# Weights of routed images one turn later, one branch for two rare cases, norms of tiles on GpSimd, constants of the scans from ScalarE's queue

## The chip, the cores and the metric

The kernel runs on one core of a Trainium2 chip. A core has five engines that run their own instruction streams side by side: TensorE (PE, matmuls; PEld are its weight loads), VectorE (DVE), ScalarE (ACT), GpSimd (POOL) and SyncE (SP, which here only issues DMAs). DMAs are issued from SP's, ACT's or POOL's queue. Each engine executes its own stream in order, so an instruction that waits for a semaphore holds up all that stand behind it on that engine. The metric is device time in microseconds from the first to the last instruction; lower is better.

## The reference

Two layers over an image batch `x` of shape (4, 256, 32, 32), all in float32. Each layer adds a token mixer to `x`, then a mixture of experts. The first layer's mixer is attention that keeps, in each row, only the `dyn_k` largest of 1024 scores; its mixture has 8 experts of 256 by 256, two for each token. The second layer's mixer is a selective scan in four directions; its experts are 256 by 1024. What matters here:

```python
attn = jnp.where(ranks < dyn_k, attn, -jnp.inf)
attn = jax.nn.softmax(attn, axis=-1)
...
rw, re = jax.lax.top_k(probs, TOP_K)
rw = rw / jnp.maximum(rw.sum(-1, keepdims=True), 1e-12)
...
h = jax.nn.gelu(tokens @ w1[e] + b1[e], approximate=False)
y = h @ w2[e] + b2[e]
out = out + combine[:, e:e + 1] * y
...
t = t + _L0_ffn_ref(_ln_t(t), ...)
```

`tokens` are layer-normalised rows; the two weights of a token come from the two largest router logits.

## The kernel before

**Order of stages.** (1) Attention of four images, with the first mixture's routing beside it; (2) a seam with two branches that are hardly ever taken; (3) the first mixture in 36 tiles of 256 tokens of one expert; (4) the scans; (5) the second mixture; (6) the output.

**Attention.** A half is 128 query rows of one group of four heads; there are 64. The loop `for i in range(len(order) + 8)` calls `turn(i)`; in a turn four halves stand at different steps (half i gets its scores, half i-3 its window and its masks), and one quarter of the weights of a pair of halves is exponentiated and multiplied with the values. The whole loop stands under `tc.manual_schedule()` (L1162): every engine gets its instructions in the order in which the code emits them. Work that is not of a half (projections, convolution, the routing) is cut into steps by generators. `plan(first, needed, steps, places)` enters them with a first place and a due turn, and `beside(i, place)`, called at five places of a turn, emits the next step of the one that is begun or due first. A step that yields True has put matmuls into the single PSUM bank of `bank(name)`; the next step reads them.

**Masks.** `Half.mask` (L810) makes four masks of 128x1024 on POOL (L814) in a turn. The matmuls of `Pair.weights` (L874) add them to the scores of both halves of a pair. After the masks POOL has `verify`, then whatever `behind_masks(i)` (L941) emits.

**Routing beside attention.** For images 0 to 2, `Routing0` starts its turns at `turn0 = 16 b + 24`. `feed` and `count` are planned steps. In turn 1 and 2 `spread` and `root` compute variance and reciprocal root on POOL (L290 to L311). `share` (L321, ACT, called in `before_masks` of turn 3) exponentiates the difference of two logits times that root. `shares` (L324, DVE) and `locate` (L331 to L337, POOL), in `behind_masks` of turn 3, make weights and slots; `fix` (L340, DVE, turn 4) rounds the slots; `send` (L212) writes one tile of 128 tokens a turn in turns 5 to 12 with two indirect DMAs from POOL, each of which waits for the one before.

**The last image** goes through `halved(b, h, ...)` for two halves of 512 tokens, and then `table` (L418 to L459, DVE), which lays out tiles: which expert and which block. The same function `halved` is used again in the first rare case. It reads: choose two experts (L361 to L380), count them by matmuls (`counted`), positions (L388 to L396), reciprocal root by three Newton steps (L397 to L403), Exp on ACT (L404), weights (L405 to L410); then eight sends for each half from POOL.

**The seam.** `bad` (L1387 to L1391) tests whether any row's threshold was ambiguous; `tc.If(again > 0)` (L1394) repeats attention by bits. Then constants are loaded (L1417 on ACT's queue; L1612 to L1617 five of the scans on SP's), b1 and b2 of the experts on SP's queue (L1812, L1814), and `tc.If(more_tiles > 0)` (L1901) runs tiles beyond 36. An If is a block that every engine passes; outside the manual part a scheduler orders the work between such blocks, in program order where things are ready.

**Tiles of the first mixture** (`Tile0`, from L1823): `load` (SP: rows xs, w1, w2), `normed` (L1846), `turned` (four transposes, L1853, one copy L1855), `small` (L1860 to L1871), `hidden` (eight matmuls L1878, Gelu L1880), `result` (eight matmuls L1886, L1889), `store` (L1893, L1895, and a DMA from POOL, L1897). Norms have two buffers (`pb`, bufs=2):

```python
nc.scalar.activation(self.xn[:, a], self.xs[:, a, :C], AF.Identity,
                     bias=self.xs[:, a, C + 3 : C + 4], scale=self.xs[:, a, C + 4 : C + 5])
```

Beside the tiles, six steps after each: from tile 14 on the 16 gathers of image 0's results (`fetched`, L1763, indirect DMAs from POOL), their transposes (`completed`), and the preparation of the scans (`Prep.steps`); from tile 22 on the gathers of image 1. In the scans and the rest nothing is changed.

Of the kernel before, what the change touches and what calls it, by code (L numbers as in the profile page):

```python
# [11 lines left out]
F32 = mybir.dt.float32  # L12
F16 = mybir.dt.float16
BF16 = mybir.dt.bfloat16
I32 = mybir.dt.int32
# [47 lines left out]
def metaformer(ctx: ExitStack, tc: tile.TileContext, t: dict, out: bass.AP):  # L63
# [123 lines left out]
    extra = cons.tile([1, 1], I32, tag="extra", name="extra")  # L187
    edges = cons.tile([P, PHASES, E], F32, tag="edges", name="edges")
# [153 lines left out]
    def halved(b, h, space, bank, wide_bank):  # L342
# [7 lines left out]
        ve, nm, rr, r0, red, m1, m2 = (room([M]) for _ in range(7))  # L350
# [17 lines left out]
        def best(value, hot):  # L368
# [7 lines left out]
        nc.vector.tensor_scalar(xr[b][:, four, C], red, -1.0, float(E), ALU.mult, ALU.add)  # L376
# [8 lines left out]
        yield True  # L385
        half = NHALF * b + h
        base = bases[:, half - 1] if half else region
        nc.vector.scalar_tensor_tensor(place_, sums[:, : M * E].rearrange("p (n e) -> p n e", e=E), float(C),  # L388
                                       base.unsqueeze(1).to_broadcast(wide), ALU.mult, ALU.add)
        nc.vector.scalar_tensor_tensor(bases[:, half], sums[:, NT * E : (NT + 1) * E], float(C), base,  # L390
                                       ALU.mult, ALU.add)
        yield False
        for k, hot in enumerate((hot1, hot2)):
            nc.vector.tensor_tensor(eq, hot, place_, ALU.mult)
            nc.vector.tensor_reduce(red, eq, AX.X, ALU.add)
            nc.vector.tensor_copy(here[:, k], red)  # L396
# [8 lines left out]
        nc.vector.scalar_tensor_tensor(xr[b][:, four, C + 3], nm, C ** 0.5, ve, ALU.mult, ALU.mult)  # L405
        nc.vector.tensor_copy(xr[b][:, four, C + 4], ve)
        nc.vector.tensor_scalar(red, m2, 1.0, None, ALU.add)
        nc.vector.reciprocal(m1, red)
        nc.vector.tensor_tensor(xr[b][:, four, C + 2], m2, m1, ALU.mult)
        nc.vector.tensor_tensor(xr[b][:, four, C + 1], m1, xr[b][:, four, C + 2], ALU.subtract)  # L410
        yield None

    def table(space, bank):
# [18 lines left out]
        nc.vector.tensor_scalar(extra, ends[0:1, V - 1 :], USUAL + 0.5, None, ALU.is_gt)  # L432

# [33 lines left out]
    with ExitStack() as st:  # L467
# [473 lines left out]
        def behind_masks(i):  # L941
            for turn0, routing in routings.items():
                at = i - turn0
                if at == 1:
                    routing.spread((0, 1))
                if at == 2:
                    routing.spread((2, 3))
                    routing.root()
                if at == 3:
                    routing.shares()  # L950
                    routing.locate()
                if at == 4:
                    routing.fix()
                if 5 <= at < 13:
                    send(routing.b, (at - 5,), None)

        def before_masks(i):
            for turn0, routing in routings.items():
                if i - turn0 == 3:
                    routing.share()  # L960

# [422 lines left out]
    bad = cons.tile([1, 1], I32, tag="bad", name="bad")  # L1384
    with tc.tile_pool(name="g_ps", bufs=1, space=PSUM) as pool_p, tc.tile_pool(name="g_sb", bufs=1) as pool_s:
        sure = pool_s.tile([P, 1], F32, tag="sure", name="sure")
        nc.vector.tensor_reduce(sure, fine, AX.XY, ALU.add)  # L1387
        nc.vector.tensor_scalar(sure, sure, 2.0 * (2 * B * NT) * 4 - 0.5, None, ALU.is_ge)
        tot = pool_p.tile([P, 1], F32, tag="tot", name="tot")
        nc.tensor.matmul(tot, mean_w, sure, start=True, stop=True)  # L1390
        nc.vector.tensor_scalar(bad, tot[0:1], (P - 0.5) / C, None, ALU.is_lt)  # L1391
    again = nc.values_load(bad[0:1, 0:1], min_val=0, max_val=1,
                           skip_runtime_bounds_check_because="a comparison gives 0 or 1")
    with tc.If(again > 0):  # L1394
        with ExitStack() as st:
            attention_by_bits(st)
        with tc.tile_pool(name="g_w", bufs=1) as pool_s, tc.tile_pool(name="g_ps", bufs=4, space=PSUM) as pool_p:
            nc.sync.dma_start(slots_x0.rearrange("(a p) c -> p a c", p=P),
                              blank(pool_s)[:, :W0].unsqueeze(1).to_broadcast([P, (E * BLOCKS + 1) * T // P, W0]))
            space = pool_s.tile([P, L], F32, tag="space", name="space")  # L1400
            for b in range(B):
                for h in range(NHALF):
                    wide_bank = pool_p.tile([P, L], F32, tag="w", name="wide_bank", bufs=2)
                    for _ in halved(b, h, space, lambda name: pool_p.tile([P, HALF], F32, tag="m", name=name),
                                    lambda: wide_bank):
                        pass
                    send(b, range(4 * h, 4 * h + 4), "scatter0_again")
            for _ in table(space, lambda name: pool_p.tile([P, HALF], F32, tag="m", name=name)):
                pass
# [202 lines left out]
    wd = load_rows(sw, "wd", C, nc.sync)  # L1612
    wbc = load_rows(sw, "wbc", 2 * NS, nc.sync)
    bd = load(sw, "bd", [P, CT], eng=nc.sync)
    dsk = load(sw, "dskip", [P, CT], eng=nc.sync)

    am = load(sw, "a_log", [P, CT, NS], eng=nc.sync)  # L1617
# [192 lines left out]
    with ExitStack() as st:  # L1810
        wp = st.enter_context(tc.tile_pool(name="m0_w", bufs=1))
        b1 = load(wp, "b1_0", [P, E, CT], eng=nc.sync)  # L1812
        b2 = wp.tile([P, E, C], F32, tag="b2_0", name="b2_0")
        nc.sync.dma_start(b2, t["b2_0"].rearrange("e d -> (e d)").partition_broadcast(P).rearrange(  # L1814
            "p (e d) -> p e d", e=E))
        pw = st.enter_context(tc.tile_pool(name="m0_e", bufs=4))
        pb = st.enter_context(tc.tile_pool(name="m0_b", bufs=2))
        ps_n = st.enter_context(tc.tile_pool(name="m0_ps_n", bufs=3, space=PSUM))
        ps1 = st.enter_context(tc.tile_pool(name="m0_ps1", bufs=1, space=PSUM))
        ps_h = st.enter_context(tc.tile_pool(name="m0_ps_h", bufs=2, space=PSUM))  # L1820
        blocks_x = slots_x0.rearrange("(k a p) c -> k p a c", a=T // P, p=P)

        class Tile0:  # L1823

            def __init__(self, i):
                self.i = i

            def register(self, k, most, engines):
                return nc.values_load(every_which[0:1, k, self.i : self.i + 1], engines=engines, min_val=0,
                                      max_val=most,  # L1830
                                      skip_runtime_bounds_check_because="the minimum with that of a count")

            def load(self):
                block = self.register(1, E * BLOCKS, [mybir.EngineType.SP])
                self.xs = pb.tile([P, T // P, W0], F32, tag="xs", name="xs", bufs=6)
                nc.sync.dma_start(self.xs, blocks_x[bass.ds(block, 1)].rearrange("o p a c -> p (o a) c"))
                e = self.register(0, E - 1, [mybir.EngineType.SP])
                self.w1 = pw.tile([P, CT, C], F32, tag="w1", name="w1")
                nc.sync.dma_start(self.w1, t["w1_0"][bass.ds(e, 1)].rearrange("o (c p) f -> p (o c) f", p=P))
                self.w2 = pw.tile([P, CT, C], F32, tag="w2", name="w2")  # L1840
                nc.sync.dma_start(self.w2, t["w2_0"][bass.ds(e, 1)].rearrange("o (c p) f -> p (o c) f", p=P))

            def normed(self):
                self.xn = pb.tile([P, T // P, C], F32, tag="xn", name="xn")
                for a in range(T // P):
                    nc.scalar.activation(self.xn[:, a], self.xs[:, a, :C], AF.Identity,  # L1846
                                         bias=self.xs[:, a, C + 3 : C + 4], scale=self.xs[:, a, C + 4 : C + 5])

            def turned(self):
                tp = ps1.tile([P, CT, T], F32, tag="tp", name="tp")  # L1850
                for a in range(T // P):
                    for c in range(CT):
                        nc.tensor.transpose(tp[:, c, ts(a, P)], self.xn[:, a, ts(c, P)], ident)  # L1853
                self.xe = pb.tile([P, CT, T], F32, tag="xe", name="xe")
                nc.vector.tensor_copy(self.xe, tp)  # L1855

            def small(self):
# [15 lines left out]
            def hidden(self):  # L1873
                hp = ps_h.tile([P, CT, T], F32, tag="hp", name="hp")
                self.hid = pb.tile([P, CT, T], F32, tag="hid", name="hid")
                for f in range(CT):
                    for c in range(CT):
                        nc.tensor.matmul(hp[:, f], self.w1[:, c, ts(f, P)], self.xe[:, c],  # L1878
                                         start=(c == 0), stop=(c == CT - 1))
# [479 lines left out]
```

## Time and profile before

| What | Value |
|---|---|
| Median of three runs (range) | 4113.35 us (4110.25 to 4118.84) |
| The profiled execution | 4111.36 us |
| Its span, granted TensorE clock | 4109.6 us, 0.876 |

The stages in the profiled execution, busy microseconds of each engine and the granted clock:

| Stretch, us from the start | Stage | PE | DVE | ACT | POOL | clock |
|---|---|---|---|---|---|---|
| 0 to 265 | start, pipeline of attention fills | 173.7 | 147.6 | 174.6 | 47.0 | 0.73 |
| 265 to 1960 | attention | 1367.0 | 1465.2 | 1479.5 | 967.6 | 0.78 |
| 1960 to 2031 | end of attention, seam | 33.2 | 32.6 | 14.0 | 18.6 | 0.70 |
| 2031 to 2253 | tiles of the first mixture | 186.8 | 145.1 | 134.8 | 72.1 | 0.95 |
| 2253 to 3521 | scans | 1228.1 | 1145.6 | 872.6 | 672.1 | 0.99 |
| 3521 to 4110 | second mixture, output | 546.3 | 104.6 | 166.3 | 94.3 | 0.96 |

Rows of the profile read thus: start in us from the span's start (in a timeline), duration, engine, line of the code, operation, what it writes and from what, shapes; in brackets the time that the engine stood idle before it, and what ended that. A row of the waits says who waited for whom: us in total, how often, the longest.

### The profile page before, as it was taken

Reading aid. Unit: us, or ns where it says so; the run is one execution under the profiler, and the core shown is the slowest. Engines: PE = TensorE matmul, PEld = TensorE weight load, DVE = VectorE, ACT = ScalarE, POOL = GpSimd, SP = SyncE. Lnnn points to the kernel's source line nnn. Section 1 sums busy time; section 2 is a strip of 40 time slices with the busy share of each in tenths; the row PEclk is TensorE's granted clock in tenths of the full one; section 3 lists DMA queues with packets and bytes.
Section 4 is the critical chain, followed back from the end, with each engine's and each line's share of the span. In section 5 each row is a group of like instructions: output and inputs, shape, how many; then the busy total and the mean of one; then the engine's idle time right before and its main releaser. Section 6 shows DMA issues by size and latency. Waiting matters only on the chain. (4 is left out here: it accounts for less than half of the span.)

```text
span 4109.6 us, 50486 instructions
## 1 busy us (share of the span) xinstructions
PE 3535.1 (86%) x17586; PEld 1968.8 (48%) x17586; DVE 3040.7 (74%) x5408; ACT 2841.7 (69%) x3798; POOL 1871.6 (46%) x1621
## 2 busy tenths in 40 slices
PE   8378878878887988775687999999999999999996
PEld 5144434434353435333465444444444434688885
DVE  2689898979997899978466899899899899411112
ACT  2889999979997999885356667667667677422222
POOL 0156454665557554756233655445445446221111
PEclk9568887778777877787798999999999999999997
DMA  9300092000000000000374434333324334555555
GB/s 295 94 1 1 1 278 66 1 1 29 12 1 1 10 18 6 1 14 11 111 225 127 134 113 131 104 105 121 114 95 127 113 107 138 182 186 185 189 193 191
DMA packets 241819, 393.78 MB, mean 96 GB/s; under 512 B 31888, under 2 KB 182160, under 8 KB 241424
## 3 DMA queue, kind: packets, MB, share of 16 engines
q1 hardware_dynamic: 218992, 340.85, 26.9%
q0 software_dynamic: 19904, 48.48, 3.7%
q8 instruction: 143, 2.34, 0.2%
q10 hardware_dynamic: 2656, 1.09, 0.1%
q14 instruction: 124, 1.02, 0.1%
HBM read 280.41 MB, written 109.94 MB: 95 GB/s over the span
## 5 line engine op out<-in xcount | busy, mean ns | idle before, releaser
L814 POOL TENSOR_SCALAR dr<-s_n,last 128x1024 bf16<-128x1024 f32 x256 | 729.6, 2865 | 760.4 <-DVE state L842 381.0
L730 ACT ACTIVATE junk_a<-s_n,state 128x1024 int8<-128x1024 f32 x448 | 515.6, 1151 | 25.5 <-DVE state L848 9.2
L2031 POOL TENSOR_TENSOR da_c<-prod,come 128x1024 f32<-128x1024 f32 x128 | 247.8, 1936 | 436.1 <-DVE h L2037 385.3
L734 DVE TENSOR_SCALAR_CACHE_REDUCE junk_v<-s_n,state 128x1024 int8<-128x1024 f32 x320 | 408.7, 1277 | 8.8
L2207 ACT ACTIVATE hid<-hp,b 128x256 f32<-128x256 f32 x288 | 134.0, 475 | 355.4 <-PE hp L2205 353.1
L781 DVE SCALAR_TENSOR_TENSOR w<-s_n,win 128x1024 f32<-128x1024 f32 x256 | 353.2, 1380 | 5.5
L784 DVE MAX8 win<-w 128x8 f32<-128x1024 f32 x256 | 314.5, 1228 | 8.8
L882 ACT ACTIVATE ex<-sT 128x1024 f32<-128x1024 f32 x256 | 247.2, 1016 | 94.7 <-PE sT L874 94.5
L1998 POOL TENSOR_TENSOR uu<-dx,bb 128x1024 f32<-128x1024 f32 x127 | 302.2, 2380 | 1.5 <-DMA bb<-bc_d 1.5
L730 ACT ACTIVATE junk_a<-s_n,guess 128x1024 int8<-128x1024 f32 x256 | 294.8, 1151 | 7.1
L2037 DVE TENSOR_TENSOR_SCAN h<-da_c,uu 128x1024 f32<-128x1024 f32 x127 | 288.9, 2275 | 0.0
L2011 DVE TENSOR_TENSOR_SCAN h<-da,uu 128x1024 f32<-128x1024 f32 x127 | 288.6, 2273 | 0.0
L2020 DVE TENSOR_TENSOR_SCAN h<-da,uu 128x1024 f32<-128x1024 f32 x127 | 287.6, 2265 | 0.0
L892 PE MATMUL o_ps<-ex,vT 128*32 128x256 f32 x2048 | 242.8, 458 | 50.4 <-ACT ex L882 41.4
L1982 ACT ACTIVATE da_c<-delta,a_log 128x1024 f32<-128x1024 f32 x128 | 267.6, 2091 | 5.3 <-DMA rows_y<-ys 5.2
L2041 PE MATMUL hp<-h,ident 128*128 128x512 f32 x512 | 250.4, 612 | 22.6 <-DVE h L2037 22.4
L2205 PE MATMUL hp<-xe,w 128*128 128x256 f32 x1152 | 258.6, 381 | 6.9 <-DVE xe L2193 6.7
L2216 DVE TENSOR_TENSOR ys<-yp,b2e 128x512 f32<-128x512 f32 x36 | 24.9, 692 | 319.1 <-PE yp L2213 319.1
L764 ACT COPY s_n<-sp 128x1024 f32<-128x1024 f32 x256 | 245.6, 1003 | 20.4 <-PE sp L756 16.3
L2218 POOL DMA_INDIRECT results<-ys,to x72 | 70.0, 972 | 409.8 <-DVE ys L2216 185.7
L2213 PE MATMUL yp<-w2e,hid 128*128 128x256 f32 x1152 | 255.9, 379 | 0.0
L2006 PE MATMUL hp<-da_c,ident 128*128 128x512 f32 x512 | 248.7, 608 | 6.4 <-POOL da_c L2031 3.7
(641 smaller groups left out, 7782.0 us busy)
## 6 DMA issues: line engine op xcount, KB each, us to landing
cb<-bc_d SPq DMA_DIRECT2D x128, 512.0 KB
bb<-bc_d SPq DMA_DIRECT2D x127, 512.0 KB
w<-in_w SPq DMA_DIRECT2D x36, 1024.0 KB
w2e<-in_w SPq DMA_DIRECT2D x36, 1024.0 KB
slots_x<-zeros SPq DMA_DIRECT2D x1, 33669.0 KB
slots_x<-zeros SPq DMA_DIRECT2D x1, 33282.0 KB
w<-in_w SPq DMA_DIRECT2D x72, 256.0 KB
xs<-slots_x SPq DMA_DIRECT2D x36, 261.0 KB
```

The lines of the kernel that those rows point to most:

```text
L730: nc.scalar.activation(junk, self.row(r), AF.Sign, bias=thr, scale=-1.0, accum_out=u)
L734: nc.vector.tensor_scalar(junk, self.row(r), thr, None, ALU.is_lt, ALU.add, accum_out=u)
L781: nc.vector.scalar_tensor_tensor(w, self.row(r), self.win[:, r, 0:1], self.row(r), ALU.is_gt if r < LAST_DVE else ALU.is_ge, ALU.subtract, ...
L784: nc.vector.max(out=self.win[:, r, 1:], in_=w)
L814: ins = nc.gpsimd.tensor_scalar(dr, self.row(r), self.last[:, r : r + 1], None, ALU.is_lt)
L1982: nc.scalar.activation(grid(self.da_c), cols_flipped(self.prep.delta[:, self.c]), AF.Exp, scale=self.decay)
L1998: nc.gpsimd.tensor_tensor(self.uu[:, 0], self.prep.dx[:, self.c], self.bb, ALU.mult)
L2011: nc.vector.tensor_tensor_scan(rows.rearrange("p r w -> p (r w)"), self.da, self.uu[:, 0], 0.0, ALU.mult, ALU.add)
L2020: nc.vector.tensor_tensor_scan(hs[:, ::-1], self.da[:, ::-1], self.uu[:, 0][:, ::-1], 0.0, ALU.mult, ALU.add)
L2037: nc.vector.tensor_tensor_scan(hs, self.da_c, self.uu[:, 1], 0.0, ALU.mult, ALU.add)
L2205: nc.tensor.matmul(hp[:, f % 2], self.w1[:, c, ts(f, P)], self.xe[:, c], start=(c == 0), stop=(c == CT - 1))
L2213: nc.tensor.matmul(yp[:, a], self.hid[:, f, ts(a, P)], self.w2[:, f, :], start=(f == 0), stop=(f == NF - 1))
```

## The change

Five edits. The steps of `Routing0` move to later turns, and image 2's sends go two tiles to a turn. In `halved`, the reciprocal root and the Exp come before the step that reads the counts; the code of the first expert goes to a tile `code` first and is written to the row at the end. The test `bad` becomes a planned step `doubts` with due turn 100.5, between the last image's halves (100 and 101). `table` computes `rare`, the sum of the two rare conditions; one `tc.If` on it holds both cases inside, each in an If of its own. `Tile0` and its pools move, unchanged but for `normed`, into a function `tiles_of_0(st, name)` that is called in the rare case and in the usual one. Five constants of the scans are loaded from ACT's queue.

```diff
@@ halved
-        nc.vector.tensor_scalar(xr[b][:, four, C], red, -1.0, float(E), ALU.mult, ALU.add)
+        nc.vector.tensor_copy(code, red)
...
         counted(sums, both, M)
-        yield True
-        half = NHALF * b + h
...
         nc.vector.tensor_scalar(ve, ve, 1e-5, None, ALU.add)
...
         nc.scalar.activation(m2, m2, AF.Exp)
+        yield True
+        half = NHALF * b + h
+        base = bases[:, half - 1] if half else region
...
+        for k, hot in enumerate((hot1, hot2)):
+            nc.vector.tensor_tensor(eq, hot, place_, ALU.mult)
+            nc.vector.tensor_reduce(red, eq, AX.X, ALU.add)
+            nc.vector.tensor_copy(here[:, k], red)
         nc.vector.tensor_scalar(red, m2, 1.0, None, ALU.add)
         nc.vector.reciprocal(m1, red)
+        nc.vector.scalar_tensor_tensor(xr[b][:, four, C + 3], nm, C ** 0.5, ve, ALU.mult, ALU.mult)
+        nc.vector.tensor_scalar(xr[b][:, four, C], code, -1.0, float(E), ALU.mult, ALU.add)
+        nc.vector.tensor_copy(xr[b][:, four, C + 4], ve)
@@ table
+        nc.vector.scalar_tensor_tensor(rare, ends[0:1, V - 1 :], USUAL + 0.5, bad, ALU.is_gt, ALU.add)
@@ behind_masks, before_masks
-                if at == 3:
+                if at == 4:
                     routing.shares()
                     routing.locate()
-                if at == 4:
+                if at == 6:
                     routing.fix()
-                if 5 <= at < 13:
-                    send(routing.b, (at - 5,), None)
+                if routing.b < B - 2 and 7 <= at < 15:
+                    send(routing.b, (at - 7,), None)
+                if routing.b == B - 2 and 7 <= at < 11:
+                    send(routing.b, (2 * at - 14, 2 * at - 13), None)
...
-                if i - turn0 == 3:
+                if i - turn0 == 4:
                     routing.share()
+        def doubts():
+            sure = p2.tile([P, 1], F32, tag="fr", name="all_sure", bufs=1)
+            nc.vector.tensor_reduce(sure, fine, AX.XY, ALU.add)
+            nc.vector.tensor_scalar(sure, sure, 2.0 * (2 * B * NT) * 4 - 0.5, None, ALU.is_ge)
+            tot = bank("tot")[:, 0:1]
+            nc.tensor.matmul(tot, mean_w, sure, start=True, stop=True)
+            yield True
+            nc.vector.tensor_scalar(bad, tot[0:1], (P - 0.5) / C, None, ALU.is_lt)
+            yield False
+
+        plan(70 * PLACES, 100.5, doubts())
@@ the seam
-    with tc.If(again > 0):
+    some = nc.values_load(rare[0:1, 0:1], min_val=0, max_val=2, ...)
+    with tc.If(some > 0):
+        redo = cons.tile([1, 1], I32, tag="redo", name="redo")
+        nc.vector.tensor_copy(redo, bad)
+        again = nc.values_load(redo[0:1, 0:1], min_val=0, max_val=1, ...)
+        with tc.If(again > 0):
...
+        with tc.If(more_tiles > 0):
+            with ExitStack() as st:
+                Tile0, _, _ = tiles_of_0(st, "mx")
...
-    wd = load_rows(sw, "wd", C, nc.sync)
-    wbc = load_rows(sw, "wbc", 2 * NS, nc.sync)
+    wd = load_rows(sw, "wd", C, nc.scalar)
+    wbc = load_rows(sw, "wbc", 2 * NS, nc.scalar)
...
-    am = load(sw, "a_log", [P, CT, NS], eng=nc.sync)
+    am = load(sw, "a_log", [P, CT, NS], eng=nc.scalar)
@@ normed
-                    nc.scalar.activation(self.xn[:, a], self.xs[:, a, :C], AF.Identity,
-                                         bias=self.xs[:, a, C + 3 : C + 4], scale=self.xs[:, a, C + 4 : C + 5])
+                    nc.gpsimd.tensor_scalar(self.xn[:, a], self.xs[:, a, :C], self.xs[:, a, C + 4 : C + 5],
+                                            self.xs[:, a, C + 3 : C + 4], ALU.mult, ALU.add)
```

## The prediction

> **What bounds the kernel now.** I read the page first, then the waits of the attention stage, the timelines of single engines at the places named there, and last the tile stage. All views are of the kernel before.
>
> ```profile
> PE 3535.1 (86%) x17586; PEld 1968.8 (48%) x17586; DVE 3040.7 (74%) x5408; ACT 2841.7 (69%) x3798; POOL 1871.6 (46%) x1621
> ```
>
> No engine is the bound over the whole span. The chain that ended last starts only at 3518 us (its last layer), so it says nothing of the places changed. Hence stage by stage. The waits between 200 and 1960 us, where attention runs (what waited, on whom: total, times, longest):
>
> ```profile
> ACT space L321 <- POOL space L308: 57.6, 3, 19.4
> POOL dr L814 <- DVE space L324: 40.5, 3, 13.5
> ```
>
> L321 is `share()`, one 0.21 us Exp, once for each of three routed images. ACT stands 57.6 us for it. The third time, in the timelines of ACT, POOL and DVE (start, duration, instruction, idle before it and who ended it):
>
> ```profile
> 1733.79 1.91 ACT L764 COPY s_n<-sp 128x1024 f32<-128x1024 f32 x2
> 1754.51 0.21 ACT L321 ACTIVATE space<-space 128x8 f32<-128x8 f32 x1 [18.82 <-POOL space L308]
> ...
> 1725.55 11.31 POOL L814 TENSOR_SCALAR dr<-s_n,last 128x1024 bf16<-128x1024 f32 x4 [5.09 <-PE sT L874]
> ...
> 1754.27 0.21 POOL L308 TENSOR_TENSOR space<-space,x 128x8 f32<-128x8 f32 x1
> ...
> 1768.70 11.32 POOL L814 TENSOR_SCALAR dr<-s_n,last 128x1024 bf16<-128x1024 f32 x4 [13.51 <-DVE space L324]
> ...
> 1761.52 0.17 DVE L768 COPY state<-guess 128x8 f32<-128x8 f32 x1 [13.21 <-ACT junk_a L730]
> ```
>
> The reader is to see a ring. POOL has the masks of turn 58 (11.3 us), then spread and root until 1754.5. ACT's Exp stands ahead of the counts of its turn; DVE waits 13.21 us for these counts; POOL's next masks wait for DVE. All three lose the time.
>
> **1. Routed weights a turn later (L960, L949 to L955).** `share` moves from turn 3 to 4, `shares` and `locate` from 3 to 4, `fix` from 4 to 6, the sends from 5 to 7. No instruction is added. Root ended at 1754.5; ACT comes to turn 60, the new place, at 1780 (its first copy), or 1761 without the stall, so 7 us stay between. What a stall costs: two turns (L768 to L768) take 40.6+29.4, 40.5+29.4 and 41.4+29.3 us at the three stalls (from 807.5, 1265.0 and 1720.1), and 28.5+25.3 us at the same two turns of image 0 (from 365.2), which has no routing beside it. Differences 16.2, 16.1, 16.9, together 49. I take **-48**. What is late next: without the stall DVE would trigger the masks at 1768.5-18.8 = 1749.7, and POOL is free at 1755.2, 5.5 us later. These masks (first of a pair, two buffers) are needed only two turns on, so I cost that at nothing; if it counted, and only DVE's 13.2 came back, it would be 13.2-5.5 = 8 each (-24). Upper end: all 57.6. `locate` (4.3 us on POOL, 1781.6 to 1786) now follows the masks of turn 4; its scratch is wanted next by kT's copy, which for image 0's routing stands at 926.2, some 22 us after the locate would end (about 904). Hidden.
>
> **2. Four sends a turn for image 2 (L955).** Its 16 sends now fill turns 63 to 66 instead of 61 to 68 with two each. POOL at the end of attention, and PE behind it:
>
> ```profile
> 1922.67 11.31 POOL L814 TENSOR_SCALAR dr<-s_n,last 128x1024 bf16<-128x1024 f32 x4 [3.76 <-DVE last L795]
> ...
> 1935.80 1.05 POOL L212 DMA_INDIRECT slots_x<-x,sent  x1 [0.16 <-issue]
> 1939.00 0.98 POOL L212 DMA_INDIRECT slots_x<-x,sent  x1 [2.15 <-DVE rden L901]
> 1940.02 11.32 POOL L814 TENSOR_SCALAR dr<-s_n,last 128x1024 bf16<-128x1024 f32 x4
> ...
> 1951.39 0.50 PE L874 MATMUL sT<-drop,dr 128*128 128x128 bf16 x3 [2.21 <-POOL dr L814]
> ```
>
> The last masks start without idle time: POOL is the bound there, PE waits for each of them, and what follows (exps, projection, last image's routing) hangs on PE. A send behind another waits about 1.9 us and takes 0.98, so four take 1.05+3x2.9 = 9.7 us. Turn 64's masks end with their verify at 1915.2; four sends to 1924.9; masks of turn 65 to 1938.0 with verify; four sends to 1947.8; last masks from 1947.8, not 1940.0: **+8** (ends 0 and +10).
>
> **3. The last image's half (L379 to L411).** The chain for the reciprocal root, 2.3 us on DVE (2000.5 to 2002.9), moves into the 3.7 us in which DVE waits for the counts. Against it, the test for ties (`doubts`) comes, by the order of due times, between the choice of experts and these counts, in the one PSUM bank: two DVE instructions (0.18, 0.15), one matmul pair (0.56), one read (0.14), about 1.2 us ahead of the counts. After the counts remain 15 small DVE instructions instead of 26; the end comes at about 2003.1 instead of 2003.9: **-1** (ends -2.5 and +1).
>
> **4. One branch, and constants on ACT's queue (L1394, L1901, L1612).** The seam between attention and tiles, engines DVE, SP's queue, ACT, PE:
>
> ```profile
> 2011.27 0.17 DVE L459 TENSOR_TENSOR edges<-edges,region 128x16 f32<-128x16 f32 x1
> 2016.83 0.07 DVE L1423 MEMSET count<- 128x8 f32 x1 [5.38 <-DVEq L1394]
> ...
> 2026.20 0.41 SPq L1836 DMA_DIRECT2D xs<-slots_x  x1
> ...
> 2028.98 1.28 ACT L1846 ACT_TABLE_LOAD   x1 [7.12 <-DMA xs<-slots_x]
> ...
> 2030.98 1.14 PE L1853 MATMUL tp<-ident,xn 128*128 128x128 f32 x4 [20.76 <-ACT xn L1846]
> ```
>
> The first branch holds DVE 5.4 us. It stays: DVE's branch at 2012.3 lets go at 2016.1, as does PE's (3.75 us), while the short jump of the second passes DVE in 0.2 us. The Trainium skill's "Runtime: NRT & Kernel Launch", section Instruction fetch mechanics, says a taken branch beyond the fetched window stalls for a fetch. By the rule the merged, longer body keeps one such stall and saves none; by the row a second branch costs what its engines wait to meet: SP stood from 2021.1 to 2025.6, 4.5 us, DVE coming last behind the a_log constant. I follow the row. SP drops five issues (2016.35 to 2018.8) and that wait: after release it issues b1 (1.36), b2 (0.43), a register load, xs: 2.5 us instead of 9.85, so -7.3. But b2 is 1 MB, 4.2 us from issue to its last packet, and xs now queues behind it: landing about 7 us after release instead of 12.5, -5.5. ACT's queue takes the five issues (about 2.4 us, before anything of the tiles). The first norm no longer waits for a table (1.28), but Gelu's load may then show. **-6** (ends -9 and -3).
>
> **5. Norms of 36 tiles on GpSimd (L1846).** Removed from ACT: 72 of 592 ns. Added on POOL: 72 TENSOR_SCALAR of 128x256, a form the trace lacks at this size: between L657 (128x128, 709 ns) and L814 (128x1024, 2865 ns) a line gives 1.0 us, 2.0 a tile of some 4.6. What PE waited for in the stage (1990 to 2260 us), POOL in its gathers, and one pair of rows on the shared port:
>
> ```profile
> PE yp L1886 <- ACT hid L1880: 11.1, 10, 3.3
> ...
> PE hp L1878 <- ACT hid L1880: 8.1, 16, 1.0
> ```
>
> ```profile
> 2112.43 1.04 POOL L1763 DMA_INDIRECT y<-rows_y,slot  x1 [4.16 <-DMA rows_y<-ys]
> ...
> 2206.88 4.52 POOL L1803 TENSOR_TENSOR lead_uu<-dx,held 128x1024 f32<-128x1024 f32 x1 [2.67 <-DVE dx L1736]
> ...
> 2209.11 2.31 DVE L1864 TENSOR_SCALAR best<-xs,every_expert 128x2 f32<-128x2 f32 x1
> ```
>
> Relief: ACT's 1.1 us a tile goes; of PE's 19.2 us behind `hid` I give back half, **-10** (ends 0, -22). Gathers: 16 of image 0 hold POOL from 2112.4 to 2139.9, in program order ahead of later norms; two norm buffers carry PE two tiles, so tile 20 (transposed at 2126) would come near 2140 less what prep work fills: +8, and +3 for image 1, where prep covers most: **+11** (ends 0, +18). Port: "SBUF — State Buffer", section Who interferes with whom, says of a GpSimd instruction and a DVE one that needs the shared pair the later fully blocks until the first finishes. L1864 (0.23 us elsewhere) agrees: 2.31 us, until POOL ended at 2211.4. By the rule, if every norm stopped DVE throughout, 72x1.0 = 72 us. But L781 beside L814's masks runs 1.47 us on average (121 of them) against 1.28 alone, 0.19 each; 36 tiles with one or two such hits and DVE 65% busy: 7 to 14 us of DVE time, a third on the path. I follow these: **+3** (ends 0, +72). Sum of part 5: +4.
>
> **Sum.** -48+8-1-6+4 = -43. The profiled execution took 4111.4 us (span 4109.6), 2 below the median of 4113.35; the same difference from the median gives **4070**.
>
> **Rivals.**
> - *The tile loop gains too*: all 22 us of PE's waits return and norms slip ahead of gathers. -48+8-1-6-22 = -69: 4044. For: POOL is 32% busy there. Against: 20 us of gathers in a row.
> - *The stalls give half*: 8 each, POOL being late next: 4070+24 = 4094. For: POOL's 5.5 us. Against: the pair's due time.
> - *GpSimd's norms stop DVE*: slower. Place: the 36 tiles. Price 72 instead of 3: 4139. It decides from 43/36 = 1.2 us more a tile. For: the L1864 row; against: L781's.
> - *The Exp waits as before* (no slack gained by a turn): 4070+48 = 4118, no difference to be told. Against: order in attention is written out, and root ends 7 us ahead of turn 4.
>
> **Chances.** Forecast 0.60 (alone 4052 to 4088), tile loop gains 0.17, half 0.15, stopped 0.05, as before 0.03. What can be told from no change is about 0.2%, 8 us: faster 0.92, same 0.04, slower 0.04. The range takes in the second and third case: 4040 to 4100.
>
> **What would show it.** Right: no ACT wait on L308; turns 26, 42, 58 near 28 us; last masks start about 8 us after their trigger allows; xs issued 2.5 us behind the one branch; norms of about 1.0 us on POOL, a PE wait on xn in the gathers. Wrong: those turns still over 35 us, or a stage of tiles (2031 to 2253, 222 us) longer by more than 30.

## The result and the profile after

| | Time, median (range) | Against before, 95% interval |
|---|---|---|
| before, shared runs | 4111.8 us (4108.5 to 4118.8) | |
| changed | 4076.3 us (4073.3 to 4081.9) | 0.9913 [0.9896, 0.9930] |
| forecast | 4070 us (4040 to 4100) | |

The profiled execution of the changed kernel took 4081.9 us, its span is 4080.2; against the profiled execution of before the span is 29.4 us shorter. It is the slowest of the four executions of the changed kernel, so the account below shows less than the 35.5 us between the medians. I read it by the same marks as before the change.

The page first: ACT's 72 norms are POOL's now and DVE has three instructions more, everything else is there as it was.

```profile
PE 3528.6 (86%) x17586; PEld 1968.7 (48%) x17586; DVE 3043.3 (75%) x5411; ACT 2806.1 (69%) x3726; POOL 1925.6 (47%) x1693
```

The Exp of `share` (now L323), in the groups by line between 200 and 1960 us (line, what, count, busy us, mean ns, idle before it):

```profile
L323 ACT ACTIVATE space<-space 128x8 f32<-128x8 f32 x3 | 0.6, 213 | 0.0
```

The last column was 57.6 and is 0.0. The wait of POOL's masks for the shares on DVE, 40.5 us before, has no row of that window any more.

The last masks and the seam, in the timelines of POOL, SP, DVE and PE:

```profile
1895.37 0.96 POOL L214 DMA_INDIRECT slots_x<-x,sent  x1 [2.02 <-DMA slots_x<-x,sent]
1896.36 11.30 POOL L817 TENSOR_SCALAR dr<-s_n,last 128x1024 bf16<-128x1024 f32 x4
...
1967.14 0.17 DVE L462 TENSOR_TENSOR edges<-edges,region 128x16 f32<-128x16 f32 x1
...
1971.08 0.34 SPq L91 DMA_DIRECT2D b<-in_b  x1
...
1971.62 0.07 DVE L1538 MEMSET count<- 128x8 f32 x1 [4.30 <-DVEq L1495]
...
1974.24 0.40 SPq L1428 DMA_DIRECT2D xs<-slots_x  x1
...
1978.88 1.16 POOL L1438 TENSOR_SCALAR xn<-xs 128x256 f32<-128x256 f32 x2 [3.81 <-DMA xs<-slots_x]
...
1979.55 1.23 PE L1445 MATMUL tp<-ident,xn 128*128 128x128 f32 x4 [13.41 <-POOL xn L1438]
```

The fourth send of a turn stands right ahead of the last masks; xs is issued 3.2 us after SP's first issue behind the branch (9.85 before), and the first transposes start 12.2 us after the table of tiles ends (19.5 before). DVE still stands 4.3 us at the branch (5.4 before).

The tiles: waits of PE from 1960 to 2225 us, then the timelines of POOL and of PE around the gathers of image 0:

```profile
PE tp L1445 <- POOL xn L1438: 36.3, 3, 17.8
...
PE yp L1478 <- ACT hid L1472: 6.2, 2, 4.3
```

```profile
2058.65 0.55 POOL L1438 TENSOR_SCALAR xn<-xs 128x256 f32<-128x256 f32 x1 [1.37 <-PE tp L1445]
2060.48 1.08 POOL L1878 DMA_INDIRECT y<-rows_y,slot  x1 [1.28 <-DMA rows_y<-ys]
...
2085.43 1.54 POOL L1878 DMA_INDIRECT y<-rows_y,slot  x1 [0.30 <-issue]
...
2087.24 3.30 POOL L1438 TENSOR_SCALAR xn<-xs 128x256 f32<-128x256 f32 x5
```

```profile
2068.32 2.29 PE L1478 MATMUL yp<-w,hid 128*128 128x256 f32 x8
2088.44 0.69 PE L1445 MATMUL tp<-ident,xn 128*128 128x128 f32 x2 [17.84 <-POOL xn L1438]
...
2147.63 1.21 PE L1445 MATMUL tp<-ident,xn 128*128 128x128 f32 x4 [5.04 <-POOL xn L1438]
```

The reader is to see the row of 16 gathers: from 2060.5 to 2087.0 POOL does no norm; the row even cuts a tile in two, one of whose norms is done at 2059.2. PE goes on with what it has until 2070.6 and then stands 17.84 us. The other two of the three waits are the seam (13.41 us, shown above; 20.8 before) and 5.04 us behind the gathers of image 1. Before the change PE's only wait for a norm inside the tiles was 3.1 us.

The account of the profiled executions, stage by stage (my subtraction of the marks):

| Stretch | before | after | difference | forecast |
|---|---|---|---|---|
| start to turn 0 | 122.6 | 121.7 | -0.9 | 0 |
| turn 0 to turn 63 | 1753.4 | 1702.0 | -51.4 | -48 |
| turn 63 to last masks | 64.1 | 72.7 | +8.6 | +8 |
| last masks to end of table | 71.4 | 71.0 | -0.4 | -1 |
| end of table to first transposes | 19.5 | 12.2 | -7.3 | -6 |
| first transposes to first scan | 222.1 | 242.0 | +19.9 | +4 |
| scans, second mixture, output | 1856.5 | 1858.6 | +2.1 | 0 |
| sum | 4109.6 | 4080.2 | -29.4 | -43 |

### The profile page after: what moved, and what is told of

Same layout as the page of the kernel before. It is cut to its first block, busy times and chain, and to the rows that moved or that the text cites. A ratio compares the mean times of both kernels' runs of the same rounds, so it can differ in the third digit from the quotient of the medians.

```text
span 4080.2 us, 50501 instructions
## 1 busy us (share of the span) xinstructions
PE 3528.6 (86%) x17586; PEld 1968.7 (48%) x17586; DVE 3043.3 (75%) x5411; ACT 2806.1 (69%) x3726; POOL 1925.6 (47%) x1693
```

## The experiments

After the account the open point was the stage of tiles: is it the gathers, as the waits say, or GpSimd's norms by themselves, or something else that is new there? Second, are the parts independent? Two marks serve for the tiles: the time from the first to the 19th copy of xe (18 tiles, none of which stands behind a gather) and from the 19th to the 36th.

**Norms back on ScalarE.**

```diff
-                    nc.gpsimd.tensor_scalar(self.xn[:, a], self.xs[:, a, :C], self.xs[:, a, C + 4 : C + 5],
-                                            self.xs[:, a, C + 3 : C + 4], ALU.mult, ALU.add)
+                    nc.scalar.activation(self.xn[:, a], self.xs[:, a, :C], AF.Identity,
+                                         bias=self.xs[:, a, C + 3 : C + 4], scale=self.xs[:, a, C + 4 : C + 5])
```

> The changed kernel with the norms of the 36 tiles back on ScalarE, nothing else. Theory (gathers hold the GpSimd norms behind them): the stage of tiles, 242 us in the changed kernel, comes back to 220 to 226 us, the time to 4054 to 4062. Rival (the stage is longer for what is new around it, the lower granted clock or the weights' loads, not for the norms): stage 236 or more, time 4070 or more. If the norms had paid off elsewhere as forecast (-10 of relief), the first 18 tiles take 84 us again instead of 80.

Measured: 4068.2 us (0.9891 [0.9873, 0.9910]); the stage 230.1 us, the first 18 tiles 86.3, the rest 132.9. Both missed the theory's numbers toward the rival, the stage by 4 us and the time by 6. What came back is 11.9 of 19.9 us in the stage. Of the 8 us that did not, 5 lie in one place, between the 23rd and the 24th copy of xe (20.8 us against 15.8 before), where PE waits 5.2 us for gathered rows that have not landed (2.1 before); no norm is part of that. Alone the run doesn't decide.

**Norms split, and the reverse of it.** Tiles 0 to 17 on GpSimd and the rest on ScalarE, then the other way round:

```diff
+                    if self.i < FIRST + 3:          # reverse: self.i >= FIRST + 3
+                        nc.gpsimd.tensor_scalar(...)
+                    else:
+                        nc.scalar.activation(...)
```

> The changed kernel with the norms of tiles 0 to 17 on GpSimd and of tiles 18 to 35, beside and behind the gathers, on ScalarE. Theory (gathers hold the norms; where no gather stands ahead, GpSimd's norms are a relief): the first 18 tiles keep their 80 us, the rest takes what it took before the change, the stage 216 to 220 us, time 4048 to 4056, some 4 us under the kernel with all norms on ScalarE. Rival (GpSimd's norms slow VectorE over the shared port all along): half of the 20 us comes back, stage about 232, time about 4066.

> The changed kernel with the norms of tiles 0 to 17 on ScalarE and of tiles 18 to 35 on GpSimd, the reverse of the run with the split norms. Theory (all of the loss stands behind the two rows of gathers): tiles 0 to 17 take 84 to 86 us from first to last copy of xe (80.4 in the changed kernel), tiles 18 to 35 take 150 us as in it, against 130 with ScalarE's norms; time 4076 to 4084. Rival (GpSimd's norms cost VectorE something in every tile): tiles 18 to 35 under 142 us, time under 4072.

Measured: split 4050.0 us (0.9863 [0.9842, 0.9885]), its stage 221.4 (a little over the expected 216 to 220); reverse 4082.0 us (0.9931 [0.9914, 0.9947]). Busy time by stretch (us; the first row of each is tiles 0 to 18, the second the rest; columns: stretch, its length, busy PE, PEld, DVE, ACT, POOL with counts, granted PE clock, DMA share, GB/s). The kernel before:

```profile
2032.20:2116.70 84.50, 76.11 (x354) 61.18 (x354) 57.10 (x201) 53.12 (x109) 14.39 (x19) 0.98 0.76 231
2116.70:2244.10 127.40, 102.76 (x446) 75.70 (x446) 83.90 (x240) 76.08 (x130) 56.23 (x48) 0.93 0.60 168
```

Changed kernel:

```profile
1982.50:2062.90 80.40, 75.17 (x348) 61.26 (x348) 60.93 (x216) 32.16 (x68) 37.73 (x54) 0.95 0.81 241
2062.90:2213.00 150.10, 108.28 (x452) 80.44 (x452) 84.56 (x242) 60.66 (x100) 78.81 (x82) 0.85 0.54 145
```

Split norms:

```profile
1971.50:2050.80 79.30, 73.53 (x348) 59.91 (x348) 61.05 (x217) 34.66 (x73) 36.62 (x52) 0.97 0.80 244
2050.80:2180.40 129.60, 106.09 (x452) 78.90 (x452) 84.48 (x242) 76.43 (x132) 56.68 (x49) 0.91 0.59 166
```

The reverse:

```profile
1976.50:2063.00 86.50, 76.40 (x348) 61.32 (x348) 58.86 (x214) 50.14 (x103) 16.05 (x22) 0.95 0.73 223
2063.00:2210.50 147.50, 106.54 (x452) 79.26 (x452) 85.83 (x241) 60.53 (x100) 78.61 (x81) 0.86 0.53 147
```

The second column decides. In the profiles of all kernels here, 18 tiles take 79 to 82 us wherever GpSimd has the early norms, and 84.5 (before) to 87 with ScalarE's. Wherever GpSimd has all the late ones, the rest takes 147 to 151 us, and 127 to 133 with ScalarE's. The work of PE in the second rows of the last three kernels is the same (106 to 108 us); it is the waiting that differs. In the split kernel the gathers stand in a row just as long, but no norm is behind them (no run moves the gathers themselves); of PE's waits (1960 to 2195 us) the one for norms is:

```profile
PE tp L1449 <- ACT xn L1442: 3.1, 1, 3.1
```

In the reverse kernel both norms of tile 19 are done ahead of the row (by 2059.3; its head is at 2060.1), and PE still stands 16.1 us, one tile later.

The DVE column answers the question of the shared port: in the first row DVE is busy 58.9 us beside ScalarE's norms and 60.9 beside GpSimd's, 2 us in 18 tiles. The rival that GpSimd slows VectorE all along falls.

**The norms alone**, put into the kernel before (the same replacement, the other way):

> The kernel before with the norms of the 36 tiles on GpSimd, nothing else of the change. Theory (the loss comes with the norms and doesn't depend on the other parts): from first to last copy of xe 228 to 233 us against 211.9 before the change, time 4125 to 4133, slower than before. Rival (the loss needs the earlier start or the constants on ScalarE's queue): under 220 us, time 4110 to 4117.

Measured: 4122.5 us, ratio 1.0029 [1.0018, 1.0040]; first to last copy of xe 232.4 us. The 20.5 us are there without any other part of the change; the whole time rose by 12.4, less than expected, but it rose.

**Routing alone**, in the kernel before, with image 2's rows two a turn:

```diff
-                if at == 3:
+                if at == 4:
                     routing.shares()
                     routing.locate()
-                if at == 4:
+                if at == 6:
                     routing.fix()
-                if 5 <= at < 13:
-                    send(routing.b, (at - 5,), None)
+                if 7 <= at < 15:
+                    send(routing.b, (at - 7,), None)
...
-                if i - turn0 == 3:
+                if i - turn0 == 4:
                     routing.share()
```

> The kernel before with the routing steps alone moved (weights, roots and sends one or two turns later, image 2's sends two a turn over turns 63 to 70), nothing else of the change. Theory (each of the three stalls cost its whole length, and nothing else of the change bears on attention): 51 to 53 us less than before, 4057 to 4062; no ScalarE wait on the roots. With image 2 sent two a turn nothing is given back at the end. Rival (part of the 51 us came from the reordered half or the single branch): 4070 or more.

Measured: 4061.8 us (0.9883 [0.9863, 0.9903]), turn 0 to 63 in 1701.8 us, 64.4 us more to the last masks. The median is 47 us under that of the kernel before, where 51 to 53 were expected. With the rows two a turn, this one part gives as much as the whole change or more (0.9883 against 0.9913; the intervals just overlap).

**Image 2's rows two a turn**, in the changed kernel:

```diff
-                if routing.b < B - 2 and 7 <= at < 15:
+                if 7 <= at < 15:
                     send(routing.b, (at - 7,), None)
-                if routing.b == B - 2 and 7 <= at < 11:
-                    send(routing.b, (2 * at - 14, 2 * at - 13), None)
```

> The changed kernel with image 2's rows sent two a turn over turns 63 to 70, as the other images' are, instead of four a turn over 63 to 66. Theory (four sends ahead of the last masks hold these masks): the last masks start 64 us behind turn 63 instead of 72.7, time 4066 to 4070, 8 us less. Rival (what is late is the last image's own chain, or the eight sends left over then stand ahead of the last image's sends): no gain, 4074 to 4080, last rows sent later than before.

Measured: 4071.2 us (0.9905 [0.9888, 0.9922]). From turn 63 to the last masks 64.0 us instead of 72.7, and POOL's row shows two sends ahead of them:

```profile
1880.81 1.05 POOL L214 DMA_INDIRECT slots_x<-x,sent  x1 [0.16 <-issue]
1884.19 0.98 POOL L214 DMA_INDIRECT slots_x<-x,sent  x1 [2.33 <-DVE rden L904]
1885.20 2.87 POOL L817 TENSOR_SCALAR dr<-s_n,last 128x1024 bf16<-128x1024 f32 x1
```

The place is shown. In the whole time the gain is not: 0.9905 and 0.9913 have intervals that overlap, and the median lies just above the expected range.

**Constants back on SP's queue** (`nc.scalar` to `nc.sync` in five loads; the single branch stays):

> The changed kernel with the five constants of the scans back on the DMA queue of SyncE; the single branch stays. From the last instruction of the table of tiles to the first copy of xe passed 20.8 us before the change and 15.2 after it. Theory as forecast (five issues 2.5 us, the second branch's meeting 4.5, less what the 1 MB constant takes): 17 to 18.5 us, so that the branch gave about half. Rival (the branch alone gave it, the queue nothing): 15 to 16. Rival (the queue alone): 20 or more. The whole time moves by no more than 5 us, less than a run's spread.

Measured: from the end of the table to the first copy of xe 18.5 us, between 15.2 and 20.7: the queue gives 3.3, the branch 2.2. The two other kernels with two branches (the norms alone, routing alone) took 19.8 and 19.7, so the branch's share is known only as 1.2 to 2.2. To the issue of xs it is 10.9 us, between 6.9 in the changed kernel and 13.6 to 14.8 with two branches. The time was 4083.0 us (0.9937 [0.9920, 0.9953]), 6.7 us over the changed kernel's where 5 at most were expected; the intervals overlap.

**Both losses taken back.** Norms of tiles 18 to 31 on ScalarE, the others on GpSimd, image 2's rows two a turn:

> The changed kernel with the norms of tiles 18 to 31 on ScalarE, all others on GpSimd, and image 2's rows sent two a turn over turns 63 to 70. Theory (the two losses are independent and each is taken back in full): last masks 64 us behind turn 63, first to last copy of xe 206 to 209 us, time 4038 to 4046, under every other kernel here. Rival (they cover each other): no better than the split norms alone, 4050.

Measured: 4054.3 us (0.9864 [0.9848, 0.9881]); 63.8 us to the last masks and 207.9 from first to last copy of xe, both as expected, but the time missed its 4038 to 4046 and is not under the split norms' 4050. The expected number had started from the fastest of the split kernel's four runs. The stretch shows one thing more: the norms of the last four tiles, with no row of gathers left ahead of them, are GpSimd's again and cost nothing (tiles from the 19th copy on 126.2 us, against 129.6 to 131.8 with the split norms). Hence a pair on one chip: the split kernel again, and the split kernel with the sends alone.

> The split norms once more, beside the next kernel on one chip, since the two kernels with split norms came out alike in time (4050 and 4054) where their stages differ by 10 us. Theory (the start of attention varies by 10 us between executions of every kernel and hid the difference): 4046 to 4056.

> The changed kernel with the norms of tiles 0 to 17 on GpSimd, the rest on ScalarE, and image 2's rows sent two a turn: the split norms and this one edit. Theory (the 8 us before the last masks are real): 64 us from turn 63 to the last masks, the median 5 to 10 us under the split norms' of the same call. Rival (what the last masks gain is lost again in the time that the profile doesn't single out): the same median within 3 us.

Measured: 4054.8 us (0.9865 [0.9845, 0.9886]) and 4051.9 us (0.9860 [0.9838, 0.9882]). Turn 63 to the last masks took 71.6 and 63.7 us, turn 63 to the end of the span 2235.4 and 2229.6. So the 8 us are won at their place and some 6 are left at the end, but the medians differ by 3 us, which is the rival's number, and over all runs with split norms the sends can't be told from no difference. The stretch from turn 0 to 63, which these kernels share with the changed one, took 1695.5 to 1706.0 us in their profiles: a spread wide enough to hide it. The best kernels here stand at 0.986, the change at 0.991.

## Why the prediction was right, and where not

The time lies 6 us above the forecast, well inside the range; the likeliest case was the right one. That it came so near is in part luck: in the profiles the saving is 29.4 us of the 43 forecast, one step being 16 us off, and it is the medians, 35.5 us apart, that bring it back to 6. By its steps:

1. *Routed weights a turn later*, -48: right, cause and size. No wait on the root is left, turns 26, 42 and 58 take 29.2, 29.0 and 26.6 us (forecast near 28). The -51.4 of the two profiles is not better known than -48: over ten profiled runs with the routing moved, turn 0 to 63 took 1700.2 us on average, over the two without it 1748.2. The rival "the stalls give half" falls: the routing alone brought 47 us, about the 48 forecast for all three.
2. *Four sends a turn*, +8: right; 8.6, and two a turn take it away.
3. *The last half*, -1: not shown. From the last masks to the end of the table took 70.0 to 71.4 us in the three profiled kernels with the old order and 70.7 to 71.8 in the nine with the new one. The order was not the one I had reckoned with: the test's matmul runs at 1947.4, before the choice of experts (1950.0) and not between it and the counts, and the chain for the root then waits 2.26 us for the variance that ScalarE sums. From the last projection on DVE to the table the new order is shorter (13.0 to 14.3 us against 14.1 to 15.8), but the way from the last masks to that projection is longer (48.9 to 51.3 against 48.1 to 48.4). I have not found why.
4. *One branch, constants on ACT's queue*, -6: 7.3 less, of which some 1.5 come from the first norm's no longer being ScalarE's (12.2 us to the first transposes; 13.7 in the kernel with all norms back there). The split of it was off: I gave the branch's meeting 4.5 us and the issues 2.5, before the landing behind the 1 MB constant took some of both. At the issue of xs the runs give the branch 2.7 to 3.9 and the queue 4; at the first copy of xe 1.2 to 2.2 and 3.3 are left. So the row's 4.5 us were too much. But the reading of fetch stalls alone, which the prediction took from the Trainium skill ("Runtime: NRT & Kernel Launch", section Instruction fetch mechanics) and by which the merged branch saves nothing, makes the saving too small.
5. *Norms on GpSimd*, +4: this is the step that was wrong, by 16 of the 20 us that the stage grew. The term was the gathers, "two norm buffers carry PE two tiles, so tile 20 [...] would come near 2140 less what prep work fills: +8, and +3 for image 1". Measured: the tiles behind the 19th copy took 150.1 us instead of 127.4, +22.7, nearly all of it at the first row, where a gap of 26.2 us stands for the 5.9 of before. Two things of the term failed. PE ran on for 10.1 us behind the head of the row (2060.5 to 2070.6), not for 13.6 (2112.4 to 2126). And prep work filled nothing of the rest. Its first matmuls, in the view of their line (count, min/median/max in ns, first and last start), before and after:

```profile
L1776 PE MATMUL op<-ident,y x32: 272/273/421, 2134.1 to 2223.5; 128*128 128x128 f32 x32
...
L1891 PE MATMUL op<-ident,y x32: 272/283/421, 2100.3 to 2188.6; 128*128 128x128 f32 x32
```

They turn the rows that the gathers fetch, but it is not the gathers that hold them: before the change they begin inside the row (2112.4 to 2139.9), 21.7 us behind its head; in the changed kernel 39.8 us behind it, 13 us after its end. What holds them is PE's own order. The code lets 24 steps, four tiles, pass after the gathers (`pause(24)` in `whole`), and a dependency in `completed` puts the first transpose behind the last matmul of the tile then under way, which by the count of steps is tile 20. So the work I had counted on to fill the hole stands behind the two tiles whose norms wait. No run moves these steps forward. For image 1 the prep of image 0 is there, and its row costs little, as forecast: PE's 5.04 us, and 2.4 us more from the 20th copy of xe to the last. The relief, forecast at -10, was 4.1 us (84.5 to 80.4 in the first 18 tiles; 4.8 between the means of all profiles with ScalarE's and with GpSimd's early norms). The port, +3, is not more than that: 2 us of DVE's time in 18 tiles. The upper case that I had built on the rule of the full block (the Trainium skill, "SBUF — State Buffer", section Who interferes with whom), every norm stopping DVE throughout, would be some 20 by estimate (36 norms of 0.6 us); the rule itself holds only for a DVE instruction that needs the shared pair. A norm took 0.60 us at the median, not the 1.0 of the estimate; POOL's own load was never the trouble, its order was.

The rival of the other side, GpSimd's norms stopping VectorE, was put at 4139. Its sign would have been right for the norms alone, 4122.5 against 4110.1; its mechanism is not what did it.

The scans took 1265.1 to 1265.8 us in the kernels whose last tiles have GpSimd's norms and 1262.5 to 1264.2 in the others. I have not found why.

## What to carry to other kernels

An in-order queue that holds long rows of transfers is a poor place for a short operation on which a busy engine depends: ask not what share of the engine is free, but how long the longest row ahead of the operation is, and whether the work that should fill the hole stands, in the busy engine's own order, ahead of the instruction that will wait. Moving work for a part of the loop only, the part without such rows, keeps the gain and leaves the loss. When several edits go in together, measure each alone: here the moved routing alone came out at 0.988 of the time, all five edits at 0.991.

## What the runs showed of the hardware that was not expected

PE comes back slowly from a wait. After the 17.84 us the four matmuls of `hp` took 2.08 us, where they took 1.13 before it, and the granted clock, 1.00 up to 2070.5, was 0.56 from there to 2088.4, 0.50 to 2092.0, 0.86 to 2096.0 and then 1.00 again:

```profile
2067.35 1.13 PE L1470 MATMUL hp<-xe,w 128*128 128x256 f32 x4 [0.41 <-ACT hid L1472]
...
2089.91 2.08 PE L1470 MATMUL hp<-xe,w 128*128 128x256 f32 x4 [0.78 <-DVE xe L1447]
```

The gap between two copies of xe was 26.2 us there against 4.3 in the pace before, 21.9 more, 4 more than the wait itself.

A single norm on GpSimd can be far longer than its median of 0.60 us. By the line's own view (min, median and max in ns):

```profile
L1438 POOL TENSOR_SCALAR xn<-xs x72: 544/600/4467, 1978.9 to 2204.9; 128x256 f32<-128x256 f32 x72
```

The longest lies where VectorE ran eight operations on two tensors of 128x512 almost without a gap (2172.2 to 2177.5); that the one stretched the other is my reading of their overlap, and no run isolates it. All five kernels with a GpSimd norm at this place show it (4.27 to 4.82 us); where the norms there are ScalarE's, in the split kernel and in the one with both losses taken back, no GpSimd norm takes more than 0.95 us.
